# Attention and a non-local block on one core: a third product of q and k by seven smaller ones, k's maxima in theta/phi, and another order of the last stage

## The chip, the core and the metric

The kernel runs on one core of a Trainium2 chip. The metric is the device time of one launch in microseconds (us); lower is better. All data is fp32. The engines are named as in the profile: PE is TensorE's matmul, PEld its weights load, DVE is VectorE, ACT is ScalarE, POOL is GpSimd, SP is the engine that issues most DMAs.

## The reference

Two layers over x of 8 images, 512 channels and 32 x 32 = 1024 positions. The first is attention with 8 heads of 64 channels and a residual, the second a non-local block whose batch norm takes its statistics over all images and positions:

```python
q, k, v = conv1x1(x, Wq, bq), conv1x1(x, Wk, bk), conv1x1(x, Wv, bv)   # 512 -> 512 channels each, split in 8 heads
attn = softmax(einsum('bhdn,bhdm->bhnm', q, k) * d ** -0.5)
x = x + conv1x1(einsum('bhnm,bhdm->bhdn', attn, v), Wp, bp)
g, theta, phi = three conv1x1 of x, 512 -> 256 channels
f = einsum('bcn,bdn->bcd', theta, phi) / n
z = conv1x1(einsum('bcd,bdn->bcn', f, g), W_w, W_b) + x
out = (z - mean(z)) * rsqrt(var(z) + eps) * gamma + beta             # per channel, over images and positions
```

## The kernel before, in words

**Order of the work.** `B` = 8 images go through one loop. Image b's turn is: attention(b), then q, v and k of image b+1, then the projection p(b) with its residual, theta and phi of image b in one stage, and the non-local part g, f, wf and z of image b. One such turn lasts 264.45 us in the profile. PE's matmuls are pinned to the order in which the program writes them; so are the DVE and SP instructions wrapped in `dve` and `sp`. A scheduler places the others. PSUM is four slots of 128 x 1024 (s0 to s3), which `free` hands out in turn. Blocks of 128 x 1024 come from a ring of ten (`block`), the weights from two buffers (`wr`), the sums of exponentials and g from three (`w3`).

**Products by seven.** Every projection is a product of two matrices cut in 2 x 2 blocks, done by seven block products and some additions instead of eight (`seven`, lines 245 to 282, with the table `SEVEN`). The block products need sums of the weights' blocks, kept in DRAM after the first image, and sums of the data's blocks, t1 to t4 (`data_sums`, `more_sums`). A block product of q, k or p is 4 matmuls of 128 x 512 with their result in one PSUM slot. The first result that goes to a quarter of the output is copied from PSUM by ACT with its bias (line 360), later ones are added by DVE (line 293).

For q and k of images 1 to 7 and p of images 1 to 6, two of the seven block products, numbers 1 and 2 (`INNER`), are themselves done by seven: `nested` (lines 228 to 243) yields one 128 x 256 matmul at a time. The other five are in the table `FIVE`, 20 matmuls of 128 x 512. From the second block product on, `seven` takes one of the 14 nested matmuls after each large one (`next(steps, None)`). Each nested matmul writes a quarter of a PSUM slot, and ACT (line 353) or DVE (line 293) reads it at once. The nested products need sums of the data's quarter blocks (`inner_sums`, four subtractions of 128 x 256) and sums of the weights, which `keep_inner` makes once.

**Attention.** 64 steps per image, each with 4 matmuls for the scores (line 430), an exponential on ACT (line 433) and, two steps behind, 4 matmuls for the output (line 456). DVE adds the exponentials up in acc (line 439). At the end of each group of 8 steps the sum is folded over the partitions: `together` (lines 467 to 469) writes four parts onto one another by DMA, one from SP and three accumulating ones from POOL. For the last image (`make_f`) the fold goes by four plain DMAs and three DVE additions (`fold_parts`), in two halves, the first of which is used at step 46. The denominators are broadcast through DRAM and multiplied into the output in v's stage of the next image.

**Maxima.** The largest absolute values of q and k (line 366, four reductions each, `peaks`) bound the scores; `bound_scores` multiplies them, has PE sum them over the heads, and sets gates on q on POOL. q's reductions run in v's stage, k's right after k, which is when p begins. `bound_scores` stands in theta/phi after its fourth product.

**Theta and phi.** `theta_phi` is one `seven` with 16 matmuls of 128 x 256 to a block product; its first reads are DVE's (line 594), its additions too (line 600).

**The end.** z of the last three images (`late_unit`) waits until the last image's f is there. For these, g and wf lie in DRAM in the meantime (`put_away`, `take_back`), and the finished z of the other images comes back (`reload`, `reload_chunks`). `last_z` goes over the four chunks oc of 128 channels: units of 4 matmuls for images 5, 7 and 6, DVE's addition and bn_stats of each, then bn_aggr and a square root (`begin`). `finish` makes scale and shift, applies them to the 8 images (DVE for the first, ACT for the rest; half and half in the last chunk) and writes each image's chunk out by a DMA of 512 KB from SP. In chunk 0 the unit of image 6 is done earlier, in p's stage, and `finish` of a chunk comes after the first addition of the next one.

Of the kernel before, what the change touches and what calls it, by code (L numbers as in the profile page):

```python
# [30 lines left out]
def unshifted(ctx: ExitStack, tc: tile.TileContext, a: dict, out: bass.AP):  # L31
# [22 lines left out]
    fold1 = ctx.enter_context(tc.tile_pool(name="fold1", bufs=1))  # L54
# [59 lines left out]
    INNER = (1, 2)  # L114
    WIDTH = 7 * C + len(INNER) * 3 * P
# [40 lines left out]
    def inner_blocks(w, name, n):  # L156

        a = w[:, INNER[n]]
        extra = rest[name][:, n * 3 * P:(n + 1) * 3 * P].rearrange("p (i f) -> p i f", i=3)
        return [a[:, 0, :P], a[:, 1, :P], a[:, 1, P:], a[:, 0, P:], extra[:, 0], extra[:, 1], extra[:, 2]]  # L160

    def keep_inner(name, w):

        for n in range(len(INNER)):
            a11, a12, a22, a21, s2, s3, s4 = inner_blocks(w, name, n)
            for to, l, r, op in ((s3, a11, a21, ALU.subtract), (a21, a21, a22, ALU.add), (s2, a21, a11, ALU.subtract),
                                 (s4, a12, s2, ALU.subtract)):
                nc.vector.tensor_tensor(to, l, r, op)
        kept[name] = dram.tile([P, WIDTH], F32, tag=f"kept_{name}", name=f"kept_{name}")
        nc.sync.dma_start(kept[name][:, :14 * w.shape[3]], w.rearrange("p i k f -> p (i k f)"))  # L170
        nc.sync.dma_start(kept[name][:, 14 * w.shape[3]:], rest[name])
# [30 lines left out]
    def inner_sums(data, which, pin=lambda ins: None):  # L202

# [3 lines left out]
        pin(nc.vector.tensor_tensor(t[:, 0], b12, b11, ALU.subtract))  # L207
        pin(nc.vector.tensor_tensor(t[:, 1], b22, t[:, 0], ALU.subtract))
        pin(nc.vector.tensor_tensor(t[:, 2], b22, b12, ALU.subtract))
        pin(nc.vector.tensor_tensor(t[:, 3], b21, t[:, 1], ALU.subtract))  # L210
        data[f"inner {which}"] = {"11": b11, "21": b21, "22": b22, **{f"t{i + 1}": t[:, i] for i in range(4)}}

# [14 lines left out]

    def nested(name, stage, w, data, tags, first, add):

        slots = [bank(tag, f"{name}_in_{tag}") for tag in tags]  # L230
        for n, (q, di, begins) in enumerate((("11", "21", False), ("21", "t4", True))):
            a, d = inner_blocks(w, stage, n), data[f"inner {di}"]
            pair = slots if n == 0 else slots[::-1]
            begun = set()
            for _, wi, di, s, reads in SEVEN:
                ps = pair[s % 2 if s < 2 else 1][:, s // 2, n * 256:(n + 1) * 256]
# [8 lines left out]
    def seven(name, w, data, positions_out, first, add, between=None, early=False,  # L245
              by_chunk=False, inner=None):
# [7 lines left out]
        steps = iter(())  # L254
# [3 lines left out]
        for n, (what, wi, di, s, reads) in enumerate(FIVE if inner else EARLY if early else SEVEN):  # L258
# [14 lines left out]
            for to_ps, at, lhsT, rhs, k in work:  # L273
# [3 lines left out]
                if n:  # L277
                    next(steps, None)
            for to, is_first in reads:
                (first if is_first else add)(to, ps)  # L280
# [64 lines left out]
    def heads_of(b, what, w, bias, data, pin=lambda ins: None, later=None, **how):  # L345
# [18 lines left out]
        def peaks():  # L364
            for c in range(CC):
                ins = nc.vector.tensor_reduce(peak[:, c:c + 1], t[:, c, :], AX.X, ALU.max, apply_absolute_value=True)
                if b == 0:
# [36 lines left out]
    def attention(b, q, k, v, near_end, make_f=None):  # L404
# [66 lines left out]
        def spread(u, pin=lambda ins: None, meanwhile=lambda: None):  # L471
# [4 lines left out]
            if not make_f:  # L476
                acc = accs.pop(u).rearrange("p j n -> p (j n)")
                if u == 0:
                    folded["t"] = foldp.tile([P, 4, 1024], F32, tag="fold", name=f"fold_{b}")
                t = folded["t"]  # L480
                together(t[i * P // 4:(i + 1) * P // 4, g, :],
                         [acc[k * P // 4:(k + 1) * P // 4, :] for k in range(4)])
                if i == 3:
                    two = t[:, g, :].rearrange("(r s) n -> s r n", s=2)
                    together(t[g * D:(g + 1) * D, 2, :], [two[0], two[1]])
                if u == len(units) - 1:
                    folded["all"] = t[:, 2, :]
                return
            if i == 0:
                folded[g] = foldp.tile([P, 4, 1024], F32, tag="fold", name=f"fold_{b}_{g}")  # L490
            acc = accs.pop(u).rearrange("p j n -> p (j n)")
            for k in range(4):
                eng = nc.scalar if make_f and u == len(units) - 1 and k % 2 else nc.sync
                eng.dma_start(folded[g][i * P // 4:(i + 1) * P // 4, k, :], acc[k * P // 4:(k + 1) * P // 4, :])
            if i == 3:
                t = folded[g]
                meanwhile()
                if g == 0:
                    folded[g] = fold1.tile([P, 1, 1024], F32, tag="fold1", name=f"fold1_{b}")
                for part_of in fold_parts(g, t, pin):  # L500
                    part_of()

        def fold_parts(g, t, pin):
            return [lambda to=to, l=l, r=r: pin(nc.vector.tensor_tensor(to, l, r, ALU.add)) for to, l, r in (
                (t[:, 0], t[:, 0], t[:, 1]), (t[:, 2], t[:, 2], t[:, 3]), (folded[g][:, 0], t[:, 0], t[:, 2]))]

        def all_denominators(ps):

            t = folded.pop("all")
# [8 lines left out]
        def denominators(g, ps):  # L518

            t = folded.pop(g)  # L520
            columns(ps, folds, lambda j: t[:, 0, j * 512:(j + 1) * 512])
            alone = make_f and g == 1
            ri = (fold1.tile([P, 1, 1024], F32, tag="fold1", name=f"ri_{b}") if alone else t)[:, 0, :512]
            nc.vector.reciprocal(ri, ps)
            if alone:
# [187 lines left out]
    def late_unit(b, oc, h0=0, h1=NH, meanwhile=lambda: None):  # L713
# [9 lines left out]
        def sums():  # L723
# [3 lines left out]
            meanwhile()  # L727
# [3 lines left out]
        return sums  # L731

    def last_z():
        order = [B - LATE, B - 1, *range(B - LATE + 1, B - 1)]
        begun = None
        for oc in range(CC):
            for n, b in enumerate(order[:-1] if oc == 0 else order):
                for h0, h1 in ((0, 1), (1, 2)) if (oc, n) == (CC - 1, LATE - 1) else ((0, NH),):
                    finish_one = n == 0 and begun
                    late_unit(b, oc, h0, h1, (lambda: finish(oc - 1, *begun)) if finish_one else lambda: None)()  # L740
            begun = begin(oc)
        finish(CC - 1, *begun)
# [8 lines left out]
    def finish(oc, gs, shift):  # L751
# [4 lines left out]
        for i, b in enumerate(sorted(z)):  # L756
            t = z[b][oc]
            if i == 0 or oc == CC - 1 and i % 2 == 0:
                dve(nc.vector.tensor_scalar(t, t, gs, shift, ALU.mult, ALU.add))
            else:  # L760
                nc.scalar.activation(t, t, AF.Identity, bias=shift, scale=gs)
            nc.sync.dma_start(out_v[b, :, oc, :], t)
# [26 lines left out]
    for b in range(B):  # L789
# [5 lines left out]
        def near_end():  # L795
            if not last:
                nxt["data"] = data_sums(quarters_of(nxt["x"]), f"x_{b + 1}", (1, 2))
            elif "data" not in nxt:
# [11 lines left out]
        if not last:  # L810
            inner_sums(nxt["data"], "21", dve)
            more_sums(nxt["data"], (3, 4), dve)
            later = []
            q, peak_q = heads_of(b + 1, "q", weights("WqT"), bq, nxt["data"], dve, inner="WqT",
                                 later=later,
                                 between={1: lambda: inner_sums(nxt["data"], "t4", dve)})
# [8 lines left out]
            def sums_of_o():  # L825
                nxt["o"] = data_sums(quarters_of(o), f"o_{b}")
                if b:
                    inner_sums(nxt["o"], "21")

            k, peak_k = heads_of(b + 1, "k", weights("WkT"), bk, nxt["data"], inner="WkT", between={2: sums_of_o})  # L830
            if b:
                inner_sums(nxt["o"], "t4")
            load_w(nc.sync)
        else:
# [3 lines left out]
            between = {4: late_unit(b - 1, 0)}  # L838
# [21 lines left out]
        tp = theta_phi(b, weights("tp"), data, {} if last else {3: lambda: bound_scores(b + 1, q, k, peak_q, peak_k)})  # L860
        load_w(nc.sync)

        def before_wf():
            if last:
                z[b] = [xt[:, cc, :] for cc in range(CC)]
# [234 lines left out]
```

## Time and profile before

| | |
|---|---|
| median of 5 runs | 2156.84 us (2156.16 to 2157.45) |
| the profiled execution | 2156.66 us, span 2154.8 us |
| mean granted TensorE clock | 0.996 |
| q's stage of image 4 | 984.27 to 1007.52 us |
| k's stage of image 4 | 1032.90 to 1056.11 us |
| p, theta/phi of image 3 | from 1056.11, from 1079.32 us |
| last matmul of chunk 0 of z, image 7 | about 2102.0 us |
| first output DMA issued | 2108.28 us |

The profile is that of one execution; times inside it are from the first instruction's start. A group's line gives line, engine, operation, output from inputs with shapes, count, then busy time and mean of one, then the engine's idle time before these instructions and what ended it. PE's records are two to each matmul of the program. In a timeline line the columns are start, duration, engine, line, operation, and in brackets the idle time before it with its releaser.

### The profile page before, as it was taken

What the parts mean: (1) busy time and instruction counts of PE and PEld (TensorE: products, weight loads), DVE (VectorE), ACT (ScalarE), POOL (GpSimd) and SP (SyncE); (2) the same over time, 40 slices, a digit from 0 to 9 for tenths busy, and PEclk for the clock granted to TensorE, in tenths of its full rate; (3) what the DMA queues carried; (4) which work ended last, traced back from release to release, by engine and by line L of the source; (5) the groups of instructions that cost most, each with busy time, mean ns of one, the idle gap of its engine ahead of it and who ended that gap; (6) DMA issues with size and microseconds to landing.
All of it is one profiled execution on the core that took longest, in us unless ns stands there. A gap on an engine that the chain in (4) does not pass through costs nothing.

```text
span 2154.8 us, 29726 instructions
## 1 busy us (share of the span) xinstructions
PE 2129.8 (99%) x12426; PEld 1107.6 (51%) x12426; DVE 1356.8 (63%) x1562; ACT 741.8 (34%) x848; POOL 185.2 (9%) x235
## 2 busy tenths in 40 slices
PE   9999999999999999999999999999999999999995
PEld 4534664346733567335663366633666336643462
DVE  5466656666476664766747667476673665657736
ACT  1464104641046310463105621066212652056115
POOL 0111100110001100011000100011000110000000
PEclk9999999999999999999999999999999999999998
DMA  6333433334143331433323342233434234121648
GB/s 217 128 48 56 143 152 126 49 72 123 69 130 50 74 116 68 133 50 80 107 95 111 49 95 98 93 106 50 103 140 147 42 48 133 52 64 38 226 181 351
DMA packets 52941, 226.80 MB, mean 105 GB/s; under 512 B 9664, under 2 KB 16064, under 8 KB 45248
## 3 DMA queue, kind: packets, MB, share of 16 engines
q1 hardware_dynamic: 42128, 197.82, 27.3%
q0 software_dynamic: 9184, 25.70, 9.9%
q8 instruction: 99, 1.62, 0.3%
q10 hardware_dynamic: 1488, 1.32, 0.2%
q14 instruction: 42, 0.34, 0.0%
HBM read 138.03 MB, written 45.88 MB: 85 GB/s over the span
## 4 chain that ended last, share of the span: by engine, by line
PE 98%; DVE 1%; ACT 1%; DMA 0%; issue 0%; SPq 0%
PE ps L430 20%; PE po L456 20%; PE pv L274 9%; PE ptp L274 9%; PE pp L274 7%; PE pk L274 7%; PE pq L274 6%; PE pg L274 4%; PE pf L609 3%; PE pz L274 2%; PE pq_in_s L237 2%; PE pk_in_s L237 2%; PE pp_in_s L237 2%; PE pz L720 2%; PE pwf L644 1%; DMA x<-in_x_dram 0%
## 5 line engine op out<-in xcount | busy, mean ns | idle before, releaser
L433 ACT ACTIVATE e<-ps 128x1024 f32<-128x1024 f32 x512 | 523.1, 1025 | 427.7 <-PE ps L430 421.5
L439 DVE TENSOR_TENSOR acc<-acc,e 128x1024 f32<-128x1024 f32 x384 | 470.2, 1224 | 141.9 <-ACT e L433 137.5
L456 PE MATMUL po<-e,v 64*64 64x512 f32 x4096 | 528.7, 589 | 0.7 <-ACT w_WgT L611 0.7
L430 PE MATMUL ps<-q,k 64*64 64x512 f32 x4096 | 529.1, 589 | 0.0
L456 PEld LDWEIGHTS po<-e,v 64*64 64x64 f32 x4096 | 156.5, 133 | 283.4 <-issue 275.4
L430 PEld LDWEIGHTS ps<-q,k 64*64 64x64 f32 x4096 | 155.6, 133 | 284.1 <-issue 275.0
L469 POOL DMA_DIRECT2D fold<-acc x168 | 131.1, 781 | 892.3 <-DMA fold<-acc 555.3
L437 DVE TENSOR_TENSOR acc<-e,e 128x1024 f32<-128x1024 f32 x64 | 78.4, 1225 | 139.6 <-ACT e L433 133.0
L632 ACT ACTIVATE g<-pg,gb 128x512 f32<-128x512 f32 x31 | 21.3, 688 | 383.9 <-PE pg L274 383.8
L274 PE MATMUL pv<-w_WvT,t_x 128*128 128x256 f32 x512 | 116.4, 381 | 0.0
L274 PE MATMUL ptp<-w_tp,t_x 128*128 128x256 f32 x512 | 115.0, 380 | 0.0
L274 PEld LDWEIGHTS pv<-w_WvT,t_x 128*128 128x128 f32 x512 | 96.6, 190 | 18.5 <-issue 5.7
L274 PEld LDWEIGHTS ptp<-w_tp,t_x 128*128 128x128 f32 x512 | 96.7, 190 | 12.9
L274 PE MATMUL pp<-t_o,w_WpT 128*128 128x512 f32 x208 | 100.8, 592 | 0.0
L274 PE MATMUL pq<-t_x,w_WqT 128*128 128x512 f32 x200 | 98.8, 593 | 0.5 <-DVE w_WqT L772 0.5
L274 PE MATMUL pk<-t_x,w_WkT 128*128 128x512 f32 x200 | 98.9, 592 | 0.0
L385 ACT COPY v<-pv 128x1024 f32<-128x1024 f32 x32 | 32.4, 1013 | 185.2 <-PE pv L274 185.2
L397 POOL TENSOR_SCALAR q<-q,gates 128x1024 f32<-128x1024 f32 x32 | 35.3, 1115 | 660.9 <-DVE gates L395 569.0
L274 PE MATMUL ptp<-w_tp,x 128*128 128x256 f32 x384 | 86.8, 379 | 0.0
L274 PE MATMUL pv<-w_WvT,x 128*128 128x256 f32 x384 | 86.8, 379 | 0.0
L274 PEld LDWEIGHTS pv<-w_WvT,x 128*128 128x128 f32 x384 | 73.0, 190 | 13.3 <-issue 3.6
L274 PEld LDWEIGHTS ptp<-w_tp,x 128*128 128x128 f32 x384 | 73.0, 190 | 13.3 <-issue 3.6
(187 smaller groups left out, 2193.3 us busy)
## 6 DMA issues: line engine op xcount, KB each, us to landing
fold<-acc POOLq DMA_DIRECT2D x168, 128.0 KB, 3.1
r<-den_d SPq DMA_DIRECT2D x32, 512.0 KB, 6.7
x<-in_x_dram SPq DMA_DIRECT2D x31, 512.0 KB, 5.7
w_WqT<-kept_WqT SPq DMA_DIRECT2D x7, 2176.0 KB, 8.5
w_WkT<-kept_WkT SPq DMA_DIRECT2D x7, 2176.0 KB, 8.7
w_WpT<-kept_WpT SPq DMA_DIRECT2D x6, 2176.0 KB, 8.3
w_WvT<-kept_WvT SPq DMA_DIRECT2D x7, 1792.0 KB, 7.1
w_tp<-kept_tp SPq DMA_DIRECT2D x7, 1792.0 KB, 8.3
```

Source lines behind the costliest of these rows:

```text
L237: pe(nc.tensor.matmul(ps, a[wi], d[di], start=s not in begun, stop=True, skip_group_check=True))
L274: pe(nc.tensor.matmul(to_ps, lhsT(k), rhs(k), start=(s, at) not in begun, stop=(k == nk - 1), skip_group_check=True))
L385: seven(f"pv_{b}", w, data, True, lambda q, ps: nc.scalar.copy(at(q), as_v(ps)), lambda q, ps: dve(nc.vector.tensor_tensor(at(q), at(q), a ...
L397: nc.gpsimd.tensor_scalar(q[:, p, :], q[:, p, :], gate[:, p:p + 1], 1.0, ALU.mult, ALU.mult)
L430: pe(nc.tensor.matmul(ps[c * P // 2:(c + 1) * P // 2, j, :], k[r, p, keys], q[r, p, h * 512:(h + 1) * 512], start=True, stop=True, skip_gr ...
L433: nc.scalar.activation(e, ps, AF.Exp, scale=SCALE)
L437: nc.vector.tensor_tensor(accs[u], es[u, 0], e, ALU.add)
L439: ins = nc.vector.tensor_tensor(accs[u], accs[u], e, ALU.add)
L456: pe(nc.tensor.matmul(ps[j * D:(j + 1) * D, r, :], v[keys, m, (2 * p + j) * D:(2 * p + j + 1) * D], e[keys, j, :], start=(m == 0), stop=(m ...
L469: nc.gpsimd.dma_start(to, part_of, accum_op=ALU.add)
L609: pe(nc.tensor.matmul(ps[:, c, :], tp[:, i, c * P:(c + 1) * P], tp[:, i, CI:], start=(i == 0), stop=(i == NB - 1)))
L720: pe(nc.tensor.matmul(ps[:, h - h0, :], wf[:, d, oc * P:(oc + 1) * P], g[d][:, h * 512:(h + 1) * 512], start=(d == 0), stop=(d == IC - 1), ...
```

## The change

Five edits go together.

1. `INNER` becomes a list by name. q and k have a third product by seven, number 6, which takes the block "22" of the data; p keeps two. The large products are then the four of `FOUR`: the second one is first read into both quarters 12 and 22 by ACT, and the nested product 6 is added to quarter 12. There are 16 large and 21 small matmuls. `STEPS` says how many small ones follow each large one, and `read` reads a slot whole before the small matmuls that follow its last large one.
2. Sums of the data are put behind chosen large matmuls (`fills`), pinned in DVE's order; the inner sums of x's block 22 stand in `near_end` of attention.
3. The reductions over k are put into theta/phi behind its second product, pinned, and `bound_scores` behind the fifth instead of the fourth.
4. The last image's fold goes by `together` like the other images', but for its last unit; the pool `fold1` is gone.
5. At the end, chunk 0 of image 5 is done ahead of wf, image 4's reload ahead of the second `take_back`, `finish` of a chunk directly follows `begin`, and ACT applies the scale in chunks 0 to 2 for all images, for the first in two halves with two DMAs.

```diff
-    INNER = (1, 2)
-    WIDTH = 7 * C + len(INNER) * 3 * P
+    INNER = {"WqT": (1, 6, 2), "WkT": (1, 6, 2), "WpT": (1, 2)}
+    WIDTH = 7 * C + 3 * 3 * P
...
+    FOUR = (SEVEN[0], ("s1t1", 3, "t1", 1, (("12", True), ("22", True))), ("s2t2", 4, "t2", 0, (("12", False),)),
+            FIVE[4])
+    STEPS = {2: [0] * 4 + [1] * 14, 3: [0, 0, 0, 1, 1, 2, 2, 2, 2, 2, 2, 3, 1, 1, 1, 1]}
...
-        for n, (q, di, begins) in enumerate((("11", "21", False), ("21", "t4", True))):
+        goes_to = {1: ("11", "21", False), 6: ("12", "22", False), 2: ("21", "t4", True)}
+        for n, (q, di, begins) in enumerate(goes_to[i] for i in INNER[stage]):
             a, d = inner_blocks(w, stage, n), data[f"inner {di}"]
-            pair = slots if n == 0 else slots[::-1]
+            pair = slots[::-1] if n % 2 else slots
...
-                if n:
-                    next(steps, None)
-            for to, is_first in reads:
-                (first if is_first else add)(to, ps)
+                if three and unit in (3, 7, 11):
+                    read(reads, ps)
+                for _ in range(next(counts, 0)):
+                    next(steps)
+                if unit in fills:
+                    fills[unit]()
+                unit += 1
+            if not three or n == 3:
+                read(reads, ps)
...
-            if i == 0:
-                folded[g] = foldp.tile([P, 4, 1024], F32, tag="fold", name=f"fold_{b}_{g}")
-            acc = accs.pop(u).rearrange("p j n -> p (j n)")
-            for k in range(4):
-                eng = nc.scalar if make_f and u == len(units) - 1 and k % 2 else nc.sync
-                eng.dma_start(folded[g][i * P // 4:(i + 1) * P // 4, k, :], acc[k * P // 4:(k + 1) * P // 4, :])
+            together(to[:, g, :], parts)
...
     def last_z():
         order = [B - LATE, B - 1, *range(B - LATE + 1, B - 1)]
-        begun = None
         for oc in range(CC):
-            for n, b in enumerate(order[:-1] if oc == 0 else order):
+            for n, b in enumerate(order if oc else [B - 1]):
                 for h0, h1 in ((0, 1), (1, 2)) if (oc, n) == (CC - 1, LATE - 1) else ((0, NH),):
-                    finish_one = n == 0 and begun
-                    late_unit(b, oc, h0, h1, (lambda: finish(oc - 1, *begun)) if finish_one else lambda: None)()
-            begun = begin(oc)
-        finish(CC - 1, *begun)
+                    late_unit(b, oc, h0, h1)
+            finish(oc, *begin(oc))
...
-            if i == 0 or oc == CC - 1 and i % 2 == 0:
-                dve(nc.vector.tensor_scalar(t, t, gs, shift, ALU.mult, ALU.add))
-            else:
-                nc.scalar.activation(t, t, AF.Identity, bias=shift, scale=gs)
-            nc.sync.dma_start(out_v[b, :, oc, :], t)
+            for at in (slice(0, 512), slice(512, N)) if i == 0 and oc < CC - 1 else (slice(0, N),):
+                if oc == CC - 1 and i % 2 == 0:
+                    dve(nc.vector.tensor_scalar(t[:, at], t[:, at], gs, shift, ALU.mult, ALU.add))
+                else:
+                    nc.scalar.activation(t[:, at], t[:, at], AF.Identity, bias=shift, scale=gs)
+                nc.sync.dma_start(out_v[b, :, oc, at], t[:, at])
...
             if not last:
                 nxt["data"] = data_sums(quarters_of(nxt["x"]), f"x_{b + 1}", (1, 2))
+                inner_sums(nxt["data"], "22")
...
-            more_sums(nxt["data"], (3, 4), dve)
-            later = []
+            later, of_t4 = [], []
+            fills = {4: lambda: more_sums(nxt["data"], (3,), dve), 5: lambda: more_sums(nxt["data"], (4,), dve),
+                     8: lambda: (of_t4.extend(inner_parts(nxt["data"], "t4", dve)), of_t4[0](), of_t4[1]()),
+                     9: lambda: (of_t4[2](), of_t4[3]())}
...
+            fills = {unit: lambda i=i: more_sums(nxt["o"], (i,), dve) for unit, i in ((4, 1), (6, 2), (8, 3), (12, 4))}
             if b:
+                fills[13] = lambda: (of_21.extend(inner_parts(nxt["o"], "21", dve)), of_21[0](), of_21[1]())
+                fills[14] = lambda: (of_21[2](), of_21[3]())
...
-        tp = theta_phi(b, weights("tp"), data, {} if last else {3: lambda: bound_scores(b + 1, q, k, peak_q, peak_k)})
+        tp = theta_phi(b, weights("tp"), data, {} if last else
+                       {1: later_k[0], 4: lambda: bound_scores(b + 1, q, k, peak_q, peak_k)})
...
             if last:
+                late_unit(B - LATE, 0)
                 z[b] = [xt[:, cc, :] for cc in range(CC)]
+                reload(4, mats, "o")
                 take_back(B - LATE + 1)
-                reload(4, mats, "o")
```

## The prediction

> **What bounds the kernel.** I read the page first: how long each engine is busy, then the chain of work that ended last.
>
> ```profile
> span 2154.8 us, 29726 instructions
> ## 1 busy us (share of the span) xinstructions
> PE 2129.8 (99%) x12426; PEld 1107.6 (51%) x12426; DVE 1356.8 (63%) x1562; ACT 741.8 (34%) x848; POOL 185.2 (9%) x235
> ...
> PE 98%; DVE 1%; ACT 1%; DMA 0%; issue 0%; SPq 0%
> ```
>
> TensorE (PE) is busy for 99% of the span and makes 98% of the chain. So an edit counts only if it takes matmuls away, makes PE wait, or moves the tail, where PE has already finished. Next, the timeline of one q product (image 4's, 984.27 to 1007.52), because the change rebuilds it. Columns: start, duration, engine, line, operation.
>
> ```profile
> 999.35 1.02 PE L274 MATMUL pq<-x,w_WqT 128*128 128x512 f32 x2
> 999.55 0.48 ACT L353 ACTIVATE q<-pq_in_s,bq 128x256 f32<-128x256 f32 x1
> ...
> 1000.21 0.59 PE L237 MATMUL pq_in_s<-i_t_x,w_WqT 128*128 128x256 f32 x2
> ...
> 1000.64 1.02 PE L274 MATMUL pq<-x,w_WqT 128*128 128x512 f32 x2
> 1000.84 0.47 ACT L353 ACTIVATE q<-pq_in_s,bq 128x256 f32<-128x256 f32 x1 [0.81 <-PE pq_in_s L237]
> ```
>
> Each program matmul leaves two records. A 128x512 matmul occupies PE from 999.35 to 1000.21 (0.86 us), a 128x256 one from 1000.21 to 1000.64 (0.43). The small one's reader starts 0.20 us after its slot ends (1000.64 to 1000.84). One small matmul alternates with one large, so every reader has a large matmul to hide behind. The chain gives finer means: 24.03 us for 56 records of pp is 0.8585 per large matmul, 13.81 for 64 records of ptp is 0.4315 per small one. 20 x 0.8585 + 14 x 0.4315 = 23.21 us agrees with the stage's 23.2, so PE does not wait in it.
>
> The readers' prices, from the groups by shape (after the bar: busy us, mean ns of one):
>
> ```profile
> L353 ACT ACTIVATE q<-pq_in_s,bq 128x256 f32<-128x256 f32 x28 | 13.2, 473 | 39.1 <-PE pq_in_s L237 38.5
> L293 DVE TENSOR_TENSOR q<-q,pq 128x1024 f32<-128x1024 f32 x25 | 29.8, 1217 | 3.2 <-PE pq L274 3.2
> L293 DVE TENSOR_TENSOR q<-q,pq_in_s 128x256 f32<-128x256 f32 x70 | 29.4, 420 | 64.9 <-PE pq_in_s L237 64.9
> ```
>
> Last, what PE pays when it waits for a reader. The z stage shows it: columns as in the timeline, idle time and releaser in brackets.
>
> ```profile
> 1131.81 1.41 DVE L673 SCALAR_TENSOR_TENSOR x<-pz,Wb,x 128x512 f32<-128x512 f32 x2 [0.69 <-PE pz L274]
> ...
> 1133.27 0.30 PEld L274 LDWEIGHTS pz<-tg,ws 128*128 128x128 f32 x2 [0.61 <-DVE x L673]
> 1133.33 1.07 PE L274 MATMUL pz<-tg,ws 128*128 128x512 f32 x2
> ```
>
> The reader ends at 1133.22 (1131.81 + 1.41), the weights load begins at 1133.27, the matmul at 1133.33: 0.11 us; at the wait before it in this stage it is 0.19 (1129.70 to 1129.89). I take 0.17. **A reader that gates PE costs 0.20 + its duration + 0.17.**
>
> **Part by part.**
>
> *The third product by seven (q and k, images 1 to 7: 14 products).* Removed: four large matmuls, 4 x 0.8585 = 3.43 us. Added: seven small, 7 x 0.4315 = 3.02. Gain 0.41 per product, 5.8 us in all, if PE never waits.
>
> It does. There are now 21 small matmuls beside 16 large, and the list STEPS puts three of them (steps 14, 15, 16, counted from 0) behind large matmul 11 with nothing between. They are the third product's "11", "s1t1" and "s2t2"; "11" and "s2t2" use the same PSUM slot, and ScalarE must have read the first before the second starts (the changed program has that wait, on ScalarE). From the end of step 14 to the start of step 16: 0.20 + 0.47 + 0.17 = 0.84 us; step 15 covers 0.43. PE waits 0.41 us. Behind it stand the rest of the 21 and large matmul 12.
>
> Large matmul 12 has a second wait. It accumulates into slot 0, which VectorE reads whole after matmul 11 (128x1024): 0.20 + 1.22 + 0.17 = 1.59 us after 11's end. Steps 14 to 16 cover 3 x 0.43 = 1.29, and 1.71 with the wait among them. So that wait is hidden by 0.12 us, but it is the floor: without the ScalarE wait, 1.59 - 1.29 = 0.30 of stall would still be there. Net per product: -0.41 saved, +0.41 waited, **0.0 x 14 = 0**. Bounds: nothing waited, -5.8 (the small matmuls of before start without a visible wait); VectorE behind by one 128x256 add, see below, +4.6.
>
> [...]
>
> *VectorE's load in that stage.* 17 small adds x 0.42 + 3 whole adds x 1.22 + sums of data (2 x 1.22 + 4 x 0.42) = 14.9 us of 23.2. Laid out in the pinned order, it is free 0.24 to 0.44 us before the whole read after matmul 11. The sums cost nothing by that cover; without it each 0.1 us late is 1.4 us over 14 products.
>
> *The sums moved ahead of attention's end.* Four 128x256 subtractions (4 x 0.34 = 1.4 us by their pitch) stand before the last add of acc, so the fold and its DMAs, on SP's and POOL's queues, start 1.4 us later. They are needed for the denominators in v, over 20 us on (1014.59 against 981); I find 9 us of room. Zero; bounds 0 and 7 x 1.4 if that room were gone.
>
> *Weights.* 2368 KB instead of 2176 in 14 loads: 8.5 us becomes 9.3, queued on SP. WkT is issued at 1007.71, its product starts at 1032.9. Zero; without that lead 0.8 each.
>
> *k's maxima into theta/phi.* Four reductions (two take 2.34 us, so 1.13 apart) leave the start of p, where PE did not wait: gain 0. They now stand, pinned, between VectorE's reads of theta/phi's second and third products.
>
> ```profile
> 1086.42 1.23 DVE L594 TENSOR_TENSOR tp<-ptp,tpb 128x1024 f32<-128x1024 f32 x1
> 1089.88 1.23 DVE L594 TENSOR_TENSOR tp<-ptp,tpb 128x1024 f32<-128x1024 f32 x1 [2.23 <-PE ptp L274]
> 1093.33 1.22 DVE L600 TENSOR_TENSOR tp<-tp,ptp 128x1024 f32<-128x1024 f32 x1 [2.23 <-PE ptp L274]
> ```
>
> VectorE has 2.23 us free between the first two; the reductions take 4 x 1.13 = 4.52. They run from 1087.57 to 1092.10, so the third product's read ends near 1093.33 instead of 1091.11. The fifth product reuses that slot. It was due at 1079.32 + 4 x 3.453 = 1093.13 and now starts at 1093.33 + 0.17 = 1093.50: 0.37 us, **7 images x 0.36 = +2.5 us**. Bounds: 0 (if VectorE enters 0.4 us earlier) and 7 x 1.13 = +7.9 (one reduction later). The gates follow one product later (+3.5 us); nobody needs them before the next attention.
>
> *Last image.* Its fold moves onto accumulating DMAs as in the other images, POOL takes 3 for each of seven units, and three VectorE adds go; the denominators of the first half are wanted at step 46 of 64, and I find none of it on the path: 0. z of image 5, chunk 0, ahead of wf adds no matmul: PE ends z of image 7's chunk 0 at 2102.1 either way.
>
> *The tail.* From 2108.28 on the output DMAs run without a gap:
>
> ```profile
> 2110.00:2115.00 5.00, 5.00 (x13) 2.25 (x12) 4.42 (x6) 5.00 (x5) 0.00 (x0) 1.00 1.02 405
> 2145.00:2150.00 5.00, 0.00 (x0) 0.00 (x0) 0.00 (x0) 0.00 (x0) 0.00 (x0) 0.50 1.02 406
> ```
>
> The last columns are DMA's busy share and GB/s. 16.78 MB at 405 GB/s are 41.4 us, which ends near 2150: when the first output starts decides. Before, bn_aggr ends at 2105.39, a 1.28 us add (2105.60) stands ahead of the reciprocal, and the first DMA is issued at 2108.28. Without that add the way from bn_aggr to the apply is 1.01 us, as at the last chunk (2135.93 to 2136.94); half an image takes 0.69: issue at 2107.1, 1.2 us earlier. ScalarE has the first image done by 2107.65 and the second 1.14 later, at 2108.8, while the first's 512 KB (1.3 us) are through at 2108.4: 0.4 us of gap. **-0.8 us.** Bounds: 0 and -1.2.
>
> **Sum** against the profiled execution's 2156.66 us (span 2154.8 and 1.9 around it; 0.2 us under the median of 2156.84): 2156.66 + 0 + 2.5 - 0.8 = **2158.4 us**. About 0.2%, 4.3 us, is what a measurement here can tell from no change: below 2152.5 is faster, above 2161.2 slower.
>
> **Rivals.**
> 1. *The saving is kept.* Neither wait binds: 2156.66 - 5.8 + 2.5 - 0.8 = 2152.6; with no stall in theta/phi either, 2150.1. For it: no small matmul of before shows a wait. Against: none of before has its slot's reader one small matmul ahead of it. If only the ScalarE wait is absent, the 0.30 floor stays: 2156.8, the forecast's side.
> 2. *Slower: VectorE is late for the whole read of slot 0 after matmul 11.* It has 17 small adds and the sums to do in its fixed order. One 128x256 operation more in front (0.45 where each needs the one before) less the 0.12 of slack is +0.33 per product: 2158.4 + 14 x 0.33 = 2163.0. It decides once VectorE is 0.12 us behind; above 2161.2 from 0.20 us in that stall. Against: 14.9 of 23.2 us of load.
> 3. *Theta/phi does not wait* because VectorE reaches the reductions sooner: 2155.9.
> 4. *The change does little of what it says:* the saving is all waited away (as forecast) and the outputs do not start earlier: 2159.2.
>
> **Chances.** Forecast 0.48 (within it rival 4, 2156.5 to 2160.5); rival 1 0.22, of which 0.13 under the bound; rival 2 0.22; rival 3 0.08. So faster 0.13, same 0.48 + 0.09 + 0.08 = 0.65, slower 0.22. Leaving out a tenth on each side, the range goes from 2152.0 (just past rival 1 with a tail of -1.2, 2152.2) to 2164.0, a little past rival 2.
>
> **What would show it.** q and k stages still 23.2 us long; 14 times an idle of about 0.4 us before a small weights load of pq_in_s or pk_in_s, released by ScalarE; 7 times about 0.36 before ptp, released by VectorE; image period 264.45 to 264.8; first output 1.2 us sooner after the last matmul of chunk 0. Wrong: stages of 22.8 us (rival 1), or large matmul 12 released by VectorE with over 0.5 us (rival 2).

## The result, and the profile after

The changed kernel takes 2161.7 us (median of 27 runs, 2159.85 to 2163.28) against 2156.78 (47 runs, 2155.96 to 2158.38): a ratio of 1.0021, with a 95% interval of 1.0016 to 1.0026. It is slower by 4.9 us, just past what the prediction called a difference. The forecast was 2158.4, the range 2152.0 to 2164.0. The profiled execution took 2162.44 us. Single executions with a lower clock over their whole length, one of the kernel before (3244.76 us at 0.653) and one of the run with work for PE below (2251.75 us at 0.945), are left out of the ratios.

The changed kernel's page, engines and chain:

```profile
span 2160.7 us, 30098 instructions
## 1 busy us (share of the span) xinstructions
PE 2131.5 (99%) x12510; PEld 1121.3 (52%) x12510; DVE 1401.0 (65%) x1690; ACT 744.4 (34%) x854; POOL 202.0 (9%) x256
...
PE 91%; DVE 5%; ACT 2%; DMA 1%; POOL 0%; issue 0%; SPq 0%; DVEq 0%; ACTq 0%; POOLq 0%
```

PE is still busy for 99%, but a chain that was PE for 98% now passes through DVE and ACT for 7% of its length: readers gate PE. PE's share of busy time does not show this. Where the 5.9 us of span went can be read by comparing the start of each stage in the two timelines:

| stage | span after less span before, us |
|---|---|
| image 0's q, at the start (the first 16 records take 7.25 us, 8.09 before; the wait for VectorE's sum of the weights behind them is 0.89, 0.53 before) | -0.5 |
| k of image 1, in image 0's turn, 23.21 before and 23.43 after | +0.2 |
| image 0's p, from the end of that k to theta/phi | +3.8 |
| the other 13 stages of q and k of images 1 to 7 (q 23.31, k 23.20, both within 0.02 of before) | -0.1 |
| theta/phi of images 0 to 6, 7 x 0.31 | +2.2 |
| last image, from g to the end of p | +1.0 |
| from bn_aggr of chunk 0 to the end, 50.0 before and 49.3 after | -0.7 |

The stages run from the first matmul of one to the first of the next. Most of the last image's +1.0 is p of image 7, where VectorE waits for the broadcast of the denominators (3.9 us at the longest, 3.4 before): 24.83 us here and 24.04 before. It varies from run to run, 24.03 to 24.73 in the traces below, 24.46 in the one that has only the last stage's edits; so it is not put down to the change.

**q's stage** first, the timeline of image 4 behind large matmul 11 (which starts at 1004.24):

```profile
1004.24 1.02 PE L289 MATMUL pq<-t_x,w_WqT 128*128 128x512 f32 x2
1005.10 0.59 PE L246 MATMUL pq_in_s<-t_x,w_WqT 128*128 128x256 f32 x2
1005.30 1.22 DVE L313 TENSOR_TENSOR q<-q,pq 128x1024 f32<-128x1024 f32 x1 [0.44 <-PE pq L289]
...
1005.53 1.43 PE L246 MATMUL pq_in_s<-i_t_x,w_WqT 128*128 128x256 f32 x4
1005.73 0.91 ACT L373 ACTIVATE q<-pq_in_s,bq 128x256 f32<-128x256 f32 x2 [4.91 <-PE pq_in_s L246]
1006.25 0.30 PEld L246 LDWEIGHTS pq_in_s<-i_t_x,w_WqT 128*128 128x128 f32 x2 [0.54 <-ACT q L373]
...
1006.79 1.02 PE L289 MATMUL pq<-t_x,w_WqT 128*128 128x512 f32 x2
```

This is the forecast to a few hundredths. Step 14 ends at 1005.53 and step 15 at 1005.96, where step 16 was due. ScalarE reads step 14 from 1005.73 to 1006.20; step 16 has its weights loaded only at 1006.25, and large matmul 12 starts at 1006.79, where 1004.24 + 0.86 + 3 x 0.43 = 1006.39 would be unhindered: 0.40 us. VectorE's whole read ends at 1006.52, in time by the 0.1 us that was forecast.

The waits before weights loads over the whole execution (columns: total us, times, longest; a part of each, 0.24 where nothing is late, is there in any case):

```profile
PEld pq_in_s L246 <- ACT q L373: 3.7, 7, 0.5
PEld pk_in_s L246 <- ACT k L373: 3.7, 7, 0.5
...
PEld ptp L289 <- DVE tp L601: 3.1, 7, 0.5
...
PEld pbp L187 <- POOL wp_bv L184: 2.2, 2, 1.4
```

Of these, the kernel before has only q's wait on ScalarE, and there nothing is late:

```profile
PEld pq_in_s L237 <- ACT q L360: 1.7, 7, 0.2
```

Fourteen waits on ScalarE and seven on VectorE were forecast. The last line was not. The lines left out hold 84 waits of small products' loads on VectorE, 0.26 to 0.30 us on average; they cost PE next to nothing, since 16 x 0.8585 + 21 x 0.4315 + 0.40 = 23.20 us is all of k's stage.

**Theta/phi**, VectorE's timeline of image 3:

```profile
1090.85 1.23 DVE L601 TENSOR_TENSOR tp<-ptp,tpb 128x1024 f32<-128x1024 f32 x1
1091.99 4.59 DVE L386 TENSOR_REDUCE peak_k<-k 128x1 f32<-128x1024 f32 x4
1096.49 1.22 DVE L601 TENSOR_TENSOR tp<-ptp,tpb 128x1024 f32<-128x1024 f32 x1
```

The reductions stand between two reads, as forecast; the second read ends at 1097.71, while PE's fifth product was due at 1083.74 + 13.81 = 1097.55. The stage lasts 24.71 instead of 24.39.

**Image 0's turn**, which the prediction left out. POOL sums the bias (wp_bv, line 181; 180 before) and PE multiplies it by ones (pbp) between k and p. First line: POOL's timeline of the kernel before; second: of the changed one.

```profile
251.51 0.93 POOL L180 TENSOR_SCALAR wp_bv<-w_WpT,bvc 128x256 f32<-128x256 f32 x2 [43.81 <-PE pk L274]
```

```profile
254.29 0.93 POOL L181 TENSOR_SCALAR wp_bv<-w_WpT,bvc 128x256 f32<-128x256 f32 x2 [45.62 <-PE pk L289]
```

POOL starts 2.8 us later and needs 8.9 us (7.9 before). The 1.0 us more is in two additions that now run beside an addition of VectorE. First line: POOL before; then POOL and VectorE (1.22 us when alone) in the changed kernel.

```profile
254.48 1.40 POOL L183 TENSOR_TENSOR wp_bv<-wp_bv 128x256 f32<-128x256 f32 x2
```

```profile
257.25 2.38 POOL L184 TENSOR_TENSOR wp_bv<-wp_bv 128x256 f32<-128x256 f32 x2
257.53 1.51 DVE L201 TENSOR_TENSOR t_o<-o,t_o 128x1024 f32<-128x1024 f32 x1
```

Before, POOL finished 1.6 us ahead of PE, and PE went through without a wait:

```profile
261.05 0.95 PE L186 MATMUL pbp<-ones,wp_bv 128*128 128x1 f32 x8
261.86 3.68 PE L274 MATMUL pp<-o,w_WpT 128*128 128x512 f32 x8
```

Now PE waits for it twice, as PE's timeline of the changed kernel shows:

```profile
261.97 0.61 PE L187 MATMUL pbp<-ones,wp_bv 128*128 128x1 f32 x4 [1.01 <-POOL wp_bv L184]
263.23 0.61 PE L187 MATMUL pbp<-ones,wp_bv 128*128 128x1 f32 x4 [0.66 <-POOL wp_bv L184]
263.70 5.38 PE L289 MATMUL pp<-o,w_WpT 128*128 128x512 f32 x8
```

From the end of k (260.79) to pp it is 2.9 us instead of 0.8: 2.1 us lost, near 2.8 + 1.0 - 1.6 = 2.2. The third line holds the other half of the loss: eight records of pp took 3.68 us before. The windows of the changed kernel say why (the column after the engines is the granted clock):

```profile
263.70:264.70 1.00, 1.00 (x4) 0.47 (x4) 0.80 (x2) 0.00 (x0) 0.00 (x0) 0.93 0.81 272
264.70:268.00 3.30, 3.30 (x5) 1.35 (x4) 0.69 (x1) 0.00 (x0) 0.00 (x0) 0.51 0.04 12
```

The clock is about half (0.51 from 264.70 to 268.00) for some 3.4 us after the two waits, 5.38 - 3.68 = 1.7 us of loss. Of the changed kernel's runs a third lie at 2159.9 to 2160.6 us with a mean clock of 0.996, the others at 2161.3 to 2163.3, most of them with 0.995: by this, the drop follows in some executions and not in others, and traces of both kinds are among the runs below.

In the same turn k of image 1 loses 0.2. VectorE also makes sums of p's weights there, and one weights load waits 0.37 for its read of a small product:

```profile
245.66 0.30 PEld L246 LDWEIGHTS pk_in_s<-x,w_WkT 128*128 128x128 f32 x2 [0.37 <-DVE k L313]
```

**The end.** The first output is issued 2.43 us after bn_aggr starts (2111.41 to 2113.84) instead of 3.48. What the output DMAs then do is in the changed kernel's windows (last two columns: DMA's busy share, GB/s):

```profile
2114.00:2115.00 1.00, 1.00 (x3) 0.38 (x2) 0.96 (x3) 1.00 (x2) 0.00 (x0) 1.00 0.31 117
2115.00:2116.00 1.00, 1.00 (x4) 0.52 (x3) 0.86 (x2) 1.00 (x2) 0.00 (x0) 1.00 0.99 371
2116.00:2117.00 1.00, 1.00 (x4) 0.43 (x3) 0.96 (x2) 1.00 (x2) 0.00 (x0) 1.00 0.60 238
```

They start sooner and then run dry once (0.60), where ScalarE alone brings the images and is done with the second one 1.13 us after the first (2114.52 and 2115.65); before, the share is 0.92 in the first microsecond of transfers, and 1.02 from then on:

```profile
2109.00:2110.00 1.00, 1.00 (x3) 0.40 (x3) 1.00 (x2) 1.00 (x2) 0.00 (x0) 1.00 0.92 365
```

### The profile page after: what moved, and what is told of

Read it like the earlier page. It is cut to its first block, busy times and chain, and to the rows that moved or that the text cites. A ratio compares the mean times of both kernels' runs of the same rounds, so it can differ in the third digit from the quotient of the medians.

```text
span 2160.7 us, 30098 instructions
## 1 busy us (share of the span) xinstructions
PE 2131.5 (99%) x12510; PEld 1121.3 (52%) x12510; DVE 1401.0 (65%) x1690; ACT 744.4 (34%) x854; POOL 202.0 (9%) x256
## 4 chain that ended last, share of the span: by engine, by line
PE 91%; DVE 5%; ACT 2%; DMA 1%; POOL 0%; issue 0%; SPq 0%; DVEq 0%; ACTq 0%; POOLq 0%
PE ps L450 20%; PE po L476 20%; PE pv L289 9%; PE pp L289 7%; PE pk L289 5%; PE pq L289 5%; PE ptp L289 5%; PE pg L289 4%; PE pq_in_s L246 3%; PE pk_in_s L246 3%; PE pf L616 3%; PE pz L289 2%; PE pp_in_s L246 2%; DVE peak_k L386 1%; DVE tp L601 1%; PE pwf L651 1%
## 5 line engine op out<-in xcount | busy, mean ns | idle before, releaser
L489 POOL DMA_DIRECT2D fold<-acc x189 | 147.1, 779 | 983.9 <-DMA fold<-acc 573.8
```

The source lines that it names most:

```text
L489: nc.gpsimd.dma_start(to, part_of, accum_op=ALU.add)
```

## The experiments

**Theory** after this comparison: (1) the third product by seven gains 0.41 us per product and waits 0.40 behind large matmul 11, where two readers gate PE; (2) k's reductions cost 0.31 per image; (3) the sum of the bias in image 0's turn comes too late, because its ring block is freed later, and the waits drop PE's clock; (4) the last stage is worth some 0.7. **Rivals:** VectorE is simply behind in q and k; POOL is slowed by VectorE; p is slow in image 0 for another reason than the clock; the end is bound by the transfers in any case. Times are medians, beside 2156.7 to 2156.8 of the kernel before in the same set.

### Four small matmuls behind large matmul 11

```diff
-3: [0, 0, 0, 1, 1, 2, 2, 2, 2, 2, 2, 3, 1, 1, 1, 1]
+3: [0, 0, 0, 1, 1, 2, 2, 2, 2, 2, 0, 4, 2, 1, 1, 1]
```

> The changed kernel with one list altered: large matmul 10 is followed by no small one, large matmul 11 by four (steps 12 to 15), large matmul 12 by two. Theory: the 0.41 us that each q and k product of images 1 to 7 gains is waited away behind large matmul 11, where step 16 needs ScalarE's read of step 14 (0.84 us, covered 0.43) and large matmul 12 needs VectorE's whole read (1.59 us). Four free small matmuls cover 1.73 us and step 16 has a large one ahead of it, so both waits go: 14 x 0.41 = 5.8 us, to 2155.9, q and k stages 22.8 instead of 23.2; in image 0's turn k's block for the bias sum comes free 0.86 us sooner and the end of k 0.41 sooner, up to 0.5 more. Rival A, the wait is VectorE being behind with its adds: stages stay near 23.2, time within 1.5 us of 2161.7. Rival B, only the ScalarE wait goes and the other floor of 0.30 binds: 1.6 us, 2160.1.

Measured: 2171.44 us (ratio 1.0070, 1.0057 to 1.0082), 9.7 slower than the changed kernel instead of 5.8 faster. The theory and both rivals missed. q's and k's stages are 0.84 longer each (14 x 0.84 = 11.8; image 0's turn gives some back, as PE's first wait for POOL is 0.16 there), and the timeline of this run shows the reason in VectorE's order:

```profile
1007.16 1.22 DVE L313 TENSOR_TENSOR q<-q,pq 128x1024 f32<-128x1024 f32 x1 [0.62 <-PE pq L289]
...
1008.49 0.76 DVE L313 TENSOR_TENSOR q<-q,pq_in_s 128x256 f32<-128x256 f32 x2
1008.96 0.30 PEld L246 LDWEIGHTS pq_in_s<-t_x,w_WqT 128*128 128x128 f32 x2 [1.38 <-DVE q L313]
```

The whole read of slot 0 is written, and pinned, ahead of the reads of steps 12 and 13, which now come behind it. Step 14 goes into the slot of step 12 (the small matmuls take two slots in turn), and its weights load starts 0.05 us after the first small read ends (1008.49 + 0.42 = 1008.91). I had counted what gates PE and not the queue of the engine that does the gating.

### Step 16 behind large matmul 12

```diff
-3: [0, 0, 0, 1, 1, 2, 2, 2, 2, 2, 2, 3, 1, 1, 1, 1]
+3: [0, 0, 0, 1, 1, 2, 2, 2, 2, 2, 2, 2, 2, 1, 1, 1]
```

> The changed kernel with step 16 moved behind large matmul 12: STEPS puts two small matmuls behind large matmul 11 and two behind 12. Theory: two readers gate PE after large matmul 11. Without step 16 there ScalarE's read no longer counts, but VectorE's whole read of the slot that large matmul 12 goes on with takes 1.59 us, of which two small matmuls cover only 0.86: a wait of 0.73 instead of 0.41, +0.32 per product, 14 x 0.32 = +4.4 us, to 2166.1. Rival, the wait is step 16's alone: 14 x 0.41 = 5.8 us less, to 2155.9.

Measured: 2165.92 us (1.0041, 1.0028 to 1.0055), +4.2, against +4.4 of the theory and -5.8 of the rival. Large matmul 12 itself now waits, released by VectorE:

```profile
1008.08 0.30 PEld L289 LDWEIGHTS pq<-t_x,w_WqT 128*128 128x128 f32 x2 [0.85 <-DVE q L313]
```

Each stage is 0.31 to 0.32 longer, as expected: the floor under step 16's wait is real. Moving small matmuls about cannot remove both; the slot that is read whole and used again at once has to go.

### q's large matmuls in another order

```diff
+    SPLIT = (SEVEN[0], ("s1t1", 3, "t1", 1, ()), ("s2t2", 4, "t2", 0, (("12", True),)), ("s1t1", 3, "t1", 1, ()), FIVE[4])
-    STEPS = {2: [0] * 4 + [1] * 14, 3: [0, 0, 0, 1, 1, 2, 2, 2, 2, 2, 2, 3, 1, 1, 1, 1]}
+    STEPS = {2: [0] * 4 + [1] * 14, "q": [0, 0, 0, 1, 1, 1, 1, 1, 2, 2, 2, 2, 2, 2, 2, 2], 3: [0, 0, 0, 1, 1, 2, 2, 2, 2, 2, 2, 3, 1, 1, 1, 1]}
...
+            if split and what == "s1t1":
+                parts = parts[:1] if n == 1 else parts[1:]
...
+                if split and unit == 12:
+                    read((("12", False), ("22", True)), slots[1])
```

> The changed kernel with q's large matmuls in another order, k as it is: the four of s1t1 are split, two before s2t2 and two between s2t2 and s3t3, so that slot 0 is read with two large matmuls between; quarter 12 is then first written from s2t2 by ScalarE and s1t1 added by VectorE after matmul 12; never more than two small matmuls in a row; inner sums of t4 behind matmuls 6 and 7. Theory: both waits of q's stage go, since every reader (at most 1.63 us) has 1.72 us of large matmuls or more ahead of the next use of its slot: 7 x 0.41 = 2.9 us, to 2158.8, q stages 22.8 instead of 23.2. Rival, VectorE is too far behind in its fixed order (it then has 19 reads and sums before matmul 12): the stage stays at 23.2 or more.

Measured: 2163.69 us (1.0030, 1.0018 to 1.0043), slower than the changed kernel; q's stage is 23.54 instead of 23.31 in the same count (from q's first matmul to v's). The waits behind large matmul 11 are gone, but VectorE is not the rival that took their place. The timeline of this run:

```profile
1008.93 1.26 ACT L386 ACTIVATE q<-pq,bq 128x512 f32<-128x512 f32 x2
...
1010.07 0.48 ACT L379 ACTIVATE q<-pq_in_s,bq 128x256 f32<-128x256 f32 x1
...
1010.61 0.30 PEld L247 LDWEIGHTS pq_in_s<-i_t_x,w_WqT 128*128 128x128 f32 x2 [0.77 <-ACT q L379]
```

ScalarE does the whole read of s1t1 (1.26 us) ahead of step 16's small read, and step 18 waits for that: 0.6 us. The next order pins ScalarE's reads and puts the whole read two large matmuls later:

```diff
-                if split and unit == 12:
-                    read((("12", False), ("22", True)), slots[1])
+                if split and unit in (12, 14):
+                    read((("12", False),) if unit == 12 else (("22", True),), slots[1])
...
-                nc.scalar.activation(t[:, c, q[1]], ps, AF.Identity, bias=bias[:, c:c + 1])
+                pin(nc.scalar.activation(t[:, c, q[1]], ps, AF.Identity, bias=bias[:, c:c + 1]))
```

> The run with q's large matmuls split, with one thing mended: ScalarE's reads of q are pinned in the program's order, and the whole read of s1t1 into quarter 22 comes after large matmul 14 instead of 12. Theory: in the run before, the two waits behind matmul 11 were gone, but ScalarE did that whole read (1.26 us) ahead of step 16's small one, and step 18 waited some 0.6 us for it. With the whole read moved to where no small reader of ScalarE follows closely, q's stage goes from 23.5 to about 22.9, 0.3 to 0.4 under the changed kernel: 7 x 0.35 = 2.5 us, 2159.2. Rival, another reader takes its place as the one that comes late: q's stage stays at 23.2 or more, 2161.7.

Measured: 2159.05 us (1.0012, 1.0003 to 1.0021), 2.65 under the changed kernel where 2.5 was expected; q's stage is 22.90, 0.41 shorter than 23.31. That is the saving of the third product, to the hundredth, once nothing waits for a reader. Theory (1) holds for q; k keeps its order and its 23.20. The stages give 7 x 0.41 = 2.9; the median also depends on how many executions have the drop of the clock. The traced one has PE's waits for POOL (1.03 and 0.66 us) and no slow stretch.

### k's reductions two and two

```diff
-        def peaks():
-            for c in range(CC):
+        def peaks(of=range(CC)):
+            for c in of:
...
-                       {1: later_k[0], 4: lambda: bound_scores(b + 1, q, k, peak_q, peak_k)})
+                       {1: lambda: later_k[0]((0, 1)), 2: lambda: later_k[0]((2, 3)), 4: lambda: bound_scores(b + 1, q, k, peak_q, peak_k)})
```

> The changed kernel with two of k's four reductions behind the second product of theta/phi and two behind the third, instead of four behind the second. Theory: four take 4.5 us where VectorE has 2.23 free, and PE waits 0.31 us per image for the third product's read; two take 2.27 in each gap, so the wait goes in 7 images, 2.2 us, to 2159.5, and theta/phi lasts 24.4 instead of 24.7. Rival, the wait has another cause (gates, weights of tp): theta/phi stays at 24.7, time 2161.7.

Measured: 2158.04 us (1.0009, 1.0000 to 1.0018), -3.7 where -2.2 was expected. Each theta/phi is 0.31 shorter than in the changed kernel, 7 x 0.31 = 2.2, as expected: in VectorE's timeline of this run (image 3, whose stage starts at 1080.76) the third product's read starts as the pair of reductions ends and is done at 1092.54, 2.0 us ahead of the slot's next use at 1080.76 + 13.81 = 1094.57.

```profile
1087.86 1.23 DVE L601 TENSOR_TENSOR tp<-ptp,tpb 128x1024 f32<-128x1024 f32 x1
1089.01 2.33 DVE L386 TENSOR_REDUCE peak_k<-k 128x1 f32<-128x1024 f32 x2
1091.32 1.22 DVE L601 TENSOR_TENSOR tp<-ptp,tpb 128x1024 f32<-128x1024 f32 x1
```

The other 1.5 is the clock: in this run image 0's p stage has no slow stretch, though PE waits for POOL as before (1.03 and 0.66 us). Its runs, too, fall in two groups, 2157.3 to 2158.0 and 2159.2 to 2161.1, only with the faster one in the majority, six to five. The faster group's median, 2157.9, is 2.2 under that of the changed kernel's faster third (2160.1), which is what theta/phi gives.

### Work for PE while it waits for the bias

```diff
-        ps = next_bank("pbp")[:, 0, :CC]
+        both = next_bank("pbp")
+        ps = both[:, 0, :CC]
         for oc in range(CC):
+            for _ in range((5, 0, 3, 0)[oc]):
+                pe(nc.tensor.matmul(both[:, 1, :P], heads, heads, start=True, stop=True, skip_group_check=True))
```

> The changed kernel with eight 128x128 matmuls into an unread part of the bias's PSUM slot, five ahead of the bias's first matmul and three ahead of its third, so that PE has work while it waits for POOL in image 0's turn; the waits themselves stay. Theory: the granted clock of about 0.5 from 264.7 to 268.1 follows from PE's two idle stretches (1.0 and 0.7 us); with them filled the clock stays at 1.0 and p's first product takes 3.4 us instead of 5.2: 1.7 us, to 2160.0. Rival, p's first product is slow for another reason: 2161.7 or a little more.

Measured: 2160.29 us (1.0017, 1.0008 to 1.0026), -1.4. In the profile p's start is where it was (263.67 against 263.70), theta/phi of image 0 starts 1.7 sooner, and the window over p's first product shows the full clock:

```profile
263.60:268.00 4.40, 4.40 (x12) 2.06 (x13) 2.79 (x5) 0.00 (x0) 0.00 (x0) 1.00 0.25 73
```

One trace at full clock proves little, since those of the runs with k's reductions two and two and with q's last order have it too, with both waits. What counts are the runs: nine of eleven lie at 2160.0 to 2160.6, where a third of the changed kernel's do; two lie at 2161.7 and 2161.8, and whether the clock dropped in them is not known. So in these runs the slow stretch goes with the waits, and filling them makes it rare or stops it. In the changed kernel's trace the stretch is about 3.4 us long, from 264.5 on, and what came before it was 2.9 us (260.8 to 263.7) with 1.7 us of idling and matmuls of one column. Why the clock drops in some executions and not in others, no run shows.

### The bias's sum in a buffer that is free

```diff
-        t = block("wp_bv")
+        t = w3.tile([P, 2, 512], F32, tag="acc", name="wp_bv")
```

> The changed kernel with the buffer of the summed bias (wp_bv, image 0) taken from the three acc buffers instead of the ring of ten blocks. Theory: in image 0's turn POOL starts that sum 2.8 us later than before (254.29 against 251.51), because its ring block is freed by large matmul 11 of k, which now has 14 small ones ahead of it instead of 7; PE then waits twice for it, and its clock drops for some 3 us. With a block that is free, POOL starts when the weights are there, some 10 us sooner: both waits and the slow stretch go, 4.0 us, to 2157.7. Rival: POOL's own additions got slower beside VectorE (2.38 us for two against 1.41): then at most 1 us goes, 2160.7 or more.

Measured: 2158.83 us (1.0010, 1.0001 to 1.0019), -2.9 where -4.0 was expected. POOL starts at 240.5, both waits of pbp and the slow stretch are gone, and all eleven runs have the clock of 0.996. So the late block was the cause. But 0.7 us comes back in k's stage of image 1, which lasts 24.10 against 23.43 in the changed kernel; -2.1 - 1.7 + 0.7 = -3.1 is near what was measured. POOL now works beside VectorE's adds there, and both are slower:

```profile
243.78 2.26 POOL L181 TENSOR_SCALAR wp_bv<-w_WpT,bvc 128x256 f32<-128x256 f32 x2
```

```profile
L106 DVE TENSOR_TENSOR w_WpT<-w_WpT,a_WpT 128x512 f32<-128x512 f32 x1 | 1.1, 1124 | 0.0
```

The first line is POOL's timeline (0.93 us for the same two instructions in the changed kernel), the second a group of VectorE in the window of k's stage (687 ns in the changed kernel). The rival has a share, then, in this place, and in the changed kernel the 1.0 us that POOL's additions are longer. Why the block came free late is read from the profile and not tested further: POOL starts 0.34 us after the end of large matmul 11 of k in both kernels (251.17 and 253.94), the last reader of t2, and that matmul has 14 small ones ahead of it now instead of 7, 7 x 0.43 = 3.0 us (2.8 here, as the changed execution starts that k 0.5 sooner and loses 0.2 in it).

### The last stage's edits alone, on the kernel before

```diff
-            for n, b in enumerate(order[:-1] if oc == 0 else order):
+            for n, b in enumerate(order if oc else [B - 1]):
...
-            begun = begin(oc)
-        finish(CC - 1, *begun)
+            finish(oc, *begin(oc))
```

> The kernel before with only the last stage's edits: image 5's chunk 0 ahead of wf, the reload ahead of take_back, finish directly behind begin, ScalarE alone in chunks 0 to 2 with image 0 in two halves. Theory: the first output is issued 1.2 us sooner and 0.4 us of gap is lost again, -0.8 us, to 2156.0. Rival, the transfers fill the end in any case: 2156.8, no difference.

Measured: 2156.82 us (1.0001, 0.9992 to 1.0010): nothing. The first output is issued 2.44 us after bn_aggr starts, 1.04 sooner than before, but the span from there is 49.9 against 50.0. The DMA share is 0.65, 0.76 and 0.87 in the first three microseconds, against 0.92 and then 1.02 in the kernel before: what is won at the start is lost again. In the changed kernel the same stretch is 49.3, and within 0.1 of that in all runs made from it. Why 0.6 less there, with the same order of transfers, stays open.

### Together

With the bias's buffer, the reductions two and two, and q's first split (the order in which ScalarE is late):

> The changed kernel with three edits together: q's large matmuls split as in the run before, the bias's sum in an acc buffer, k's reductions two and two. Theory, the effects add up: 2.9 for q, 2.9 as measured for the bias (2161.7 to 2158.8), 2.2 for the reductions (the 1.5 more that the run with them alone showed is the clock after the bias's wait, which is gone here): 2161.7 - 8.0 = 2153.7, ahead of the kernel before by 0.14%. Rival, one of the gains takes place only while another wait is there: 2156 or more.

Measured: 2158.22 us (1.0006, 0.9997 to 1.0015). The miss is q's: 2158.8 - 2.2 + 7 x 0.23 = 2158.2. The effects do add up.

The bias's buffer and the reductions alone, q as in the changed kernel:

> The changed kernel with the bias's sum in an acc buffer and k's reductions two and two, q as it is. Theory: 2158.8 less 2.2 is 2156.6, within 0.2 of the kernel before: all that the change lost is accounted for by these two and the clock behind the bias's wait, and the third product by seven and the last stage bring nothing. Rival, something else is lost or won too: off by more than 0.8 either way.

Measured: 2156.47 us (0.9999, 0.9990 to 1.0008), as expected, and level with the kernel before: to within a few tenths, what the change lost is in these two places and the clock behind the first.

With the last order of q as well:

> The changed kernel with the mended order of q, the bias's sum in an acc buffer and k's reductions two and two. Theory, the effects add up: 2158.8 as measured with the bias's buffer, less 2.2 for the reductions and 2.5 for q: 2154.1, ahead of the kernel before by 2.6 us (0.12%). Rival, they do not add up: 2156.6 or more.

Measured: 2153.71 us (0.9986, 0.9977 to 0.9995), 3.0 us or 0.14% under the kernel before, the fastest version here. Its page:

```profile
span 2152.1 us, 30098 instructions
## 1 busy us (share of the span) xinstructions
PE 2125.7 (99%) x12510; PEld 1121.6 (52%) x12510; DVE 1400.6 (65%) x1690; ACT 745.0 (35%) x854; POOL 204.1 (9%) x256
```

k's stage is still 23.20. The same order for k was not tried: by the program, t1 would there be read until large matmul 11, and the ring gives its block to a sum of o that k's stage makes after matmul 8.

## Why the prediction was right or wrong

- **The third product: right.** Forecast 0.0 for the 14 products; measured -0.1 in 13 of them and +0.2 in k of image 1. The two waits have the forecast sizes (0.40 for 0.41, a slack of 0.1 for 0.12), the floor under them showed when step 16 was moved (+4.2 for +4.4), and the 0.41 saved showed in q when both were removed (22.90 for 23.31); for k that was not run.
- **VectorE's load in that stage: right but for one stage.** Only in k of image 1, where sums of p's weights come on top, does VectorE hold PE up, for 0.2 us. The cover is thin, though: one whole read ahead of two small ones cost 0.84 per product.
- **k's maxima in theta/phi: right.** 2.2 for 2.5 us; the reductions started 8.25 us into the stage, as laid out, and the wait is 0.31 for 0.36.
- **The tail: in the changed kernel 0.7 for 0.8, but not shown to be for the reason given.** The first output came 1.05 sooner (1.2 forecast) and the gap behind it is there; alone on the kernel before, the same edits bring nothing.
- **What failed is the step that counted the small matmuls only by their length.** The prediction wrote that the sum for q and k was 0.0 and priced nothing in image 0's turn, and gave no reason for that. Seven more small matmuls ahead of large matmul 11 free t2's ring block 2.8 us later. In image 0's turn the bias's sum on POOL waits for that block; it had 1.6 us of slack and also takes 1.0 us longer beside VectorE. PE then stands 2.1 us longer between k and p and runs at half clock for some 3.4 us more, in most executions by their times: +2.1 and up to +1.7 us, and k of image 1 is 0.2 longer. With these 4.0 the forecast would have been 2162.4, which is the profiled execution; in part that is luck, since 0.5 less at the start and 1.0 more in the last image were not forecast either. The time lies in the range, but rival 2, whose side it fell on, is not what happened: VectorE was on time for slot 0.
- **The sign.** 4.9 us is 0.6 past the 4.3 that the chances used, less than what the clock takes in most executions. The faster third of the runs has a median of 2160.1, +0.15%, which would have been called no change.

## What to carry to other kernels

When matmuls are put ahead of others, work out what each passed one frees, a buffer as much as a result, and follow that to the engine that waits for it, in every image and in the first and last above all. Here a saving in PE's work counted only where every slot that is read whole has at least the reader's time, an estimated 1.6 us (0.20 + 1.22 + 0.17), of other matmuls before it is used again (22.90 us for q's stage instead of 23.31); to get it, change the order of the large pieces, not only the filling between them. When a wait is shifted, look at the order of the reader's own queue first: twice here a whole read moved in front of a small one that PE needed sooner.

## What the runs showed of the hardware

- Two idle stretches of PE of 1.0 and 0.66 us within 2.9 us were followed by some 3.4 us at about half the granted clock (0.51) in the traced execution of the changed kernel, and by no such stretch in two other traces with waits of 1.03 and 0.66 us (the runs with k's reductions two and two and with q's last order). By their times, two thirds of the changed kernel's runs had the drop; with eight 128x128 matmuls in the gaps at most two of eleven had it.
- POOL and VectorE were both slower in two places where they worked at once on blocks in SBUF: in k's stage of image 1 in the run with the bias's sum in a free buffer, two of POOL's instructions took 2.26 us instead of 0.93 and an addition of VectorE 1.12 instead of 0.69; in the changed kernel, two additions of POOL took 2.38 instead of 1.40 beside an addition of VectorE of 1.51 instead of 1.22.
